# A state-space convolution feeding a 4-bit FFN: filler matmuls, one late load and one kernel product moved in the lead

## Chip, cores and metric

One core of a Trainium2 chip runs the whole kernel. The metric is device time in microseconds (us) for one execution; the time of a kernel is the median of its runs. A profiled execution gives a trace, whose span runs from the first to the last instruction.

## What is computed

`x` has 32 batch rows, 64 heads and 1024 positions. Each head has a long convolution kernel, made from a diagonal state-space model with 64 states; the masked input is convolved with it, and the result goes through a gated FFN whose weights are 4-bit integers with a scale for each group of 128 inputs. The output is added to `x`.

```python
def _L0_cond_ref(u, length, log_dt, C, log_A_real, A_imag, D):
    dtA = A * dt[:, None]
    P = dtA[:, :, None] * jnp.arange(length)
    Cs = Cc * (jnp.exp(dtA) - 1.0) / A
    kernel = 2.0 * jnp.einsum('hn,hnl->hl', Cs, jnp.exp(P)).real
    u_m = u * mask[:, None, :]
    y = irfft(rfft(u_m, 2 * L) * rfft(kernel, 2 * L))[..., :L]
    y = y + u_m * D[:, None]
    return y * mask[:, None, :]

def _L0_ffn_ref(x, ...):
    gate = x2 @ Wg          # 1024 -> 2752, dequantized from 4 bits
    up = x2 @ Wu
    inter = gate * jax.nn.sigmoid(gate) * up
    return (inter @ Wd).astype(jnp.float16)

x = x + _L0_ffn_ref(_L0_cond_ref(x, ...), ...)
```

## The kernel before

**Tiling and stages.** The 64 heads are four blocks of 16. A block's convolution gives 512 rows of FFN input, on which the FFN then runs: gate and up products (`gu_one`, `gu_pair`), the gated product, and the down product (`dn_pair`). From some 60 us on, convolution heads of the next block are woven between FFN matmuls. The part before that, in which block 0 is made ready and convolved, is called the lead here; the change touches only the lead.

**From coefficients to a convolution kernel.** For a group of heads, `phase_tables` (L183 to L210) makes tables of sines: DVE computes the phases (L192 to L204), ACT takes the sine (L207) and the square (L209). `kernel_factors` (L213 to L224) turns them into two factors `e1t` and `e2t` on DVE (L218 to L223). `make_kernel` (L421) multiplies them on PE: a matmul with the tap `D` (L425), then one small float32 matmul for each head (L427), which the trace shows as two passes each. The product `kq` is split into two float16 parts `kb` by ACT (L430) and DVE (L431), and two DMAs on ACT's queue write them to `kpad` in DRAM (L433).

**Toeplitz loads.** `toeplitz` (L513) issues on SP's queue one 512 KB load for each head (L525), which reads `kpad` with overlapping rows, so that each partition holds a shifted copy of the kernel. It can't begin before the two writes of its group have landed. The destination is a piece of a tile that is free at that time, so in the profile the same load is called `w<-kpad` (heads 0 to 7 and 15), `t<-kpad` or `ihl<-kpad`.

**Input of the convolution.** Four heads share one 512 KB load of `u`. `conv_fetch` issues those of heads 0 to 15 at the very start; `conv_split` (L492) makes two float16 parts, `uh` by a cast on ACT and `ul` by a subtract on DVE (L497). For heads 16 and up `conv_load` (L500) issues the load on SP (L503), then the cast (L507) and the subtract (L510).

**One head of the convolution.** `conv_head` (L531) issues 24 matmuls (L548): eight diagonals, and for each of them high by `uh`, high by `ul`, and low by `uh`. It is a generator that yields after each diagonal, so a head has eight steps and block 0 has 128. Two heads share a PSUM tile `cq`; after the second, DVE masks it into `y` (L560), ACT casts it to `xh` (L563), and POOL, or DVE for the last pair of a block, subtracts to give `xl` (L565). The FFN products read `xh` (L664) and `xl` (L665) and rescale their accumulator between groups (`rescale_two`, L635 to L640).

**The lead, in order.** A loop over the first two groups of four heads (`for k, h0 in enumerate((0, 4))`) makes tables, factors, kernel and Toeplitz loads, then calls `busy`, then `conv_split`. `busy` issues n filler matmuls (L884) of 128x128x128 in float32, whose result nobody reads; each is two passes on PE. Heads 8 to 15 get their tables and factors behind the loop. Then block 0 is convolved, and at given steps of its 128 other work is issued: `events` maps a step to a function, `unpack_it` unpacks the first FFN weights (two SP loads `qgu` and `z`, L578 and L579, then DVE L584, POOL L590, and ACT or DVE), and `group_it` prepares heads 24 to 31. At the events, step 7 makes the kernel of heads 8 to 15 and the factors of 16 to 23, 63 issues fillers, 56 makes the gate/up scale ratios (`scale_ratios`, L405 to L419: ACT copy, then DVE L413 to L418), 87 loads `u` of heads 16 to 19, and 75 makes the kernel of heads 16 to 23. Behind block 0, `second` makes the down-projection's ratios, issues the Toeplitz loads of heads 16 to 21 and convolves heads 16 to 31.

**What sets the order.** The tile framework places each instruction in its engine's queue by priority, in about the order in which the code issues it. `mark(key, inst)` remembers an instruction, and `with after(key)` places what is issued inside it behind the remembered one on its queue. The keys `"act"`, `"dve"` and `"sp"` stand for the latest marked instruction of that engine. SP's queue and ACT's queue issue DMAs; the framework rotates eight semaphores over the DMAs of both.

Of the kernel before, what the change touches and what calls it, by code (L numbers as in the profile page):

```python
# [17 lines left out]
ALU = mybir.AluOpType  # L18
# [164 lines left out]
def phase_tables(nc, side, pool, co, cst, h0, nh):  # L183
    ts, tt, stt = nc.vector.tensor_scalar, nc.vector.tensor_tensor, nc.vector.scalar_tensor_tensor
    hs = slice(h0, h0 + nh)
    idx = cst[:, 0:64].unsqueeze(1).to_broadcast([128, nh, 64])
    per = lambda a, n: a[:, hs].unsqueeze(2).to_broadcast([128, nh, n])
    t = lambda name, n: pool.tile([128, nh, n], F32, name=name)
    off1, off2 = cst[:, 64:65], cst[:, 65:66]

    ph, pl = t("ph", 64), t("pl", 64)
    tt(ph, per(co["wh"], 64), idx, ALU.mult)  # L192
    yield
    side.tensor_tensor(pl, per(co["wl"], 64), idx, ALU.mult)
    r1, r2 = t("r1", 64), t("r2", 32)
    yield
    ts(r1, ph, off1, MAGIC, ALU.add, ALU.add)
    ts(r2, ph[:, :, 32:], off2, MAGIC, ALU.add, ALU.add)
    yield
    stt(r1, r1, MAGIC, ph, ALU.subtract, ALU.subtract)  # L200
    stt(r2, r2, MAGIC, ph[:, :, 32:], ALU.subtract, ALU.subtract)
    yield
    stt(r1, r1, off1, pl, ALU.subtract, ALU.subtract)
    stt(r2, r2, off2, pl[:, :, 32:], ALU.subtract, ALU.subtract)  # L204
    yield
    for r in (r1, r2):
        nc.scalar.activation(r, r, AF.Sin, scale=3.1415925)  # L207
    for r in (r1, r2):
        sq_op = nc.scalar.activation(r, r, AF.Square, scale=1.4142135623730951)  # L209
    return r1, r2, sq_op  # L210


def kernel_factors(nc, pool, co, xd, s1, s2, h0, nh):  # L213
# [34 lines left out]
def every(gen):  # L248
    for _ in gen:
        pass  # L250
# [8 lines left out]
class Core:  # L259
# [183 lines left out]
    def tables(self, pool, h0, nh):  # L443
        held = h0 >= 24
        steps = phase_tables(self.nc, self.nc.vector, pool, self.co, self.cst, h0, nh)
        while True:
            try:
                with self.after("dve" if held else None), self.after("act" if held else None):
                    next(steps)
            except StopIteration as done:  # L450
                self.tab, sq_op = done.value[:2], done.value[2]
                break
            self.dve(800)
            yield
        self.mark(("sq", h0), sq_op)
        self.act(5000)
        yield
        yield from self.pause(5000)
# [33 lines left out]
    def conv_split(self, k, after, last="e"):  # L492
        u, uh, ul = self.us[k]
        with self.after(("sq", after)):
            self.nc.scalar.copy(uh, u)
        with self.after((last, after)):
            self.nc.vector.tensor_tensor(ul, u, uh, ALU.subtract)  # L497
        self.us[k] = uh, ul

    def conv_load(self, h0):  # L500
        nc = self.nc
        u = self.cv.tile([128, 8, 4, B], F32, name="u", bufs=1)
        self.mark("sp", nc.sync.dma_start(u.rearrange("p c h b -> p (c h b)"), self.io["xF"][h0 // 4]))  # L503
        uh = self.cv.tile([128, 8, 4, B], F16, name="uh")
        ul = self.cv.tile([128, 8, 4, B], F16, name="ul")
        with self.after("act"):
            nc.scalar.copy(uh, u)  # L507
        self.act(1000)
        with self.after("dve"):
            nc.vector.tensor_tensor(ul, u, uh, ALU.subtract)  # L510
        self.dve(1200)
        return uh, ul
# [323 lines left out]
def tile_ssm_ffn(ctx, tc, io):  # L836
    nc = tc.nc
    c = Core(ctx, tc, io)
# [14 lines left out]
    kg = kg_stack.enter_context(tc.tile_pool(name="kg", bufs=1))  # L853
# [27 lines left out]
    def busy(h0, n):  # L881
        e1, e2 = (e.rearrange("p h n -> p (h n)") for e in c.fac[h0])
        for _ in range(n):
            nc.tensor.matmul(c.psum("wq", "b")[:, 0, :128], e1, e2, start=True, stop=True)  # L884

    for k, h0 in enumerate((0, 4)):
        every(c.tables(tables, h0, 4))
        every(c.factors(kg, h0, 4, xd[0][:, h0:h0 + 4]))
        c.make_kernel(kg, h0, 4, "b")
        for h in range(h0, h0 + 4):  # L890
            c.t0[h] = c.toeplitz(h)
        busy(h0, 8 - 4 * k)
        c.conv_split(k, h0)
    every(c.tables(kg, 8, 8))
    every(c.factors(kg, 8, 8, xd[1]))
    c.masks()
    tc.no_sync_barrier()
# [35 lines left out]
    def load_16():  # L933
        c.us[4] = c.conv_load(16)

    events = {7: kernel_8, 63: lambda: busy(4, 10), 56: ratios_gu, 87: load_16, 75: lambda: c.make_kernel(kg, 16, 8, "b")}
    for i, _ in enumerate(c.conv(0)):
        if i in events:
            with c.after("dve" if i == 56 else None):
                events[i]()  # L940
        if i in (32, 40, 48, 56, 64, 72, 104, 116, 124):
            next(unpack_it)
        if i in (80, 86, 92, 98, 104, 110):
            next(group_it)
# [175 lines left out]
```

## Time and profile before

| | us |
|---|---|
| median of 3 runs | 1079.41 (1079.26 to 1080.23) |
| the profiled execution | 1076.19 |
| its span | 1074.4 |
| PE busy in the span | 1025.0 (95%) |
| DVE, ACT, POOL busy | 804.7, 773.7, 243.9 |
| mean granted TensorE clock | 0.997 |

The profiled execution's own time is 1.8 us more than its span and 3.2 us less than the median of the runs. In a row of the timeline the first number is the start, the second the duration from the first to the last of the xN instructions in the row; in brackets stand the idle time of the engine before it and what ended it. In a table by stretches each engine has its busy time, with the number of instructions after it.

### The profile page before, as it was taken

What the parts mean: (1) busy time and instruction counts of PE and PEld (TensorE: products, weight loads), DVE (VectorE), ACT (ScalarE), POOL (GpSimd) and SP (SyncE); (2) the same over time, 40 slices, a digit from 0 to 9 for tenths busy, and PEclk for the clock granted to TensorE, in tenths of its full rate; (3) what the DMA queues carried; (4) which work ended last, traced back from release to release, by engine and by line L of the source; (5) the groups of instructions that cost most, each with busy time, mean ns of one, the idle gap of its engine ahead of it and who ended that gap; (6) DMA issues with size and microseconds to landing.
All of it is one profiled execution on the core that took longest, in us unless ns stands there. A gap on an engine that the chain in (4) does not pass through costs nothing.

```text
span 1074.4 us, 15424 instructions
## 1 busy us (share of the span) xinstructions
PE 1025.0 (95%) x5854; PEld 512.6 (48%) x5854; DVE 804.7 (75%) x938; ACT 773.7 (72%) x1031; POOL 243.9 (23%) x272
## 2 busy tenths in 40 slices
PE   3989999999899999997999999999999999999996
PEld 3867444444344445663665444444444444444442
DVE  8964888888977786678456777777778777777775
ACT  5767778787677787778577777666666667778774
POOL 0334123232332333230112112222221111102002
PEclk9999999999999999999999999999999999999998
DMA  6976321111111424455752011000000002325002
GB/s 196 332 243 211 100 69 40 40 59 40 49 50 58 139 90 156 152 180 190 238 167 99 30 38 42 20 20 20 18 13 20 20 20 79 118 72 166 37 1 79
DMA packets 52099, 99.76 MB, mean 93 GB/s; under 512 B 9524, under 2 KB 11444, under 8 KB 52024
## 3 DMA queue, kind: packets, MB, share of 16 engines
q1 hardware_dynamic: 38888, 70.09, 20.1%
q0 software_dynamic: 5280, 17.31, 4.3%
q10 hardware_dynamic: 7856, 11.37, 3.6%
q8 instruction: 46, 0.75, 0.3%
q14 instruction: 29, 0.24, 0.1%
HBM read 78.99 MB, written 19.76 MB: 92 GB/s over the span
## 4 chain that ended last, share of the span: by engine, by line
PE 81%; DVE 7%; ACT 5%; DMA 3%; issue 2%; POOL 1%; DVEq 0%; SPq 0%; ACTq 0%; POOLq 0%
PE chq L687 23%; PE chq L688 22%; PE chq L732 12%; PE chq L733 12%; PE cq L548 6%; PE chq L664 2%; PE chq L665 2%; DMA t<-kpad 2%; ACT chq L640 1%; DVE chq L618 1%; DVE v L700 1%; ACT chq L620 1%; DMA ihl<-kpad 1%; ACT sg L695 1%; POOL spill L310 0%
## 5 line engine op out<-in xcount | busy, mean ns | idle before, releaser
L687 PE MATMUL chq<-xh,w 128*128 128x512 f16 x1216 | 459.4, 379 | 7.2 <-DVE chq L618 2.1
L688 PE MATMUL chq<-xl,w 128*128 128x512 f16 x1216 | 457.6, 379 | 0.0
L618 DVE TENSOR_SCALAR chq<-chq,gur 128x1024 f32<-128x1024 f32 x261 | 333.3, 1290 | 93.4 <-PE chq L688 91.8
L620 ACT ACTIVATE chq<-chq,gur 128x1024 f32<-128x1024 f32 x285 | 304.2, 1085 | 86.9 <-PE chq L688 84.4
L640 ACT ACTIVATE chq<-chq,dnr 128x512 f32<-128x512 f32 x358 | 232.8, 661 | 68.6 <-PE chq L733 62.8
L732 PE MATMUL chq<-ihl,wd 128*128 128x512 f16 x672 | 253.0, 379 | 8.9 <-ACT chq L640 5.2
L733 PE MATMUL chq<-ihl,wd 128*128 128x512 f16 x672 | 252.9, 379 | 0.0
L637 DVE TENSOR_TENSOR chq<-chq,dnr 128x1024 f32<-128x1024 f32 x141 | 173.1, 1230 | 81.0 <-PE chq L733 80.2
L688 PEld LDWEIGHTS <-w 128*128 128x128 fp8e4 x1216 | 118.6, 98 | 154.6 <-issue 18.5
L687 PEld LDWEIGHTS <-w 128*128 128x128 fp8e4 x1216 | 118.7, 98 | 146.7 <-issue 1.1
L310 POOL TENSOR_TENSOR ihl<-v,ihl 128x512 f16<-128x512 f32 x42 | 48.3, 1150 | 364.0 <-ACT ihl L629 364.0
L733 PEld LDWEIGHTS <-wd 128*128 128x128 fp8e4 x672 | 65.4, 97 | 81.0 <-issue 18.2
L548 PEld LDWEIGHTS <-t 128*128 128x128 f16 x1152 | 81.3, 98 | 38.7 <-DMA t<-kpad 5.8
L732 PEld LDWEIGHTS <-wd 128*128 128x128 fp8e4 x672 | 65.4, 98 | 67.2 <-issue 0.8
L548 PE MATMUL cq<-uh,t 128*128 128x256 f16 (+3 forms) x720 | 91.1, 226 | 4.1 <-DMA t<-kpad 4.0
L565 POOL TENSOR_TENSOR xl<-y,xh 128x512 f16<-128x512 f32 x28 | 36.4, 1301 | 161.0 <-ACT xh L563 161.0
L548 PE MATMUL cq<-ul,t 128*128 128x256 f16 (+3 forms) x360 | 71.6, 225 | 0.0
L629 ACT CAST ihl<-v 128x512 f16<-128x512 f32 x42 | 25.9, 617 | 58.7 <-DVE v L700 55.3
L700 DVE SCALAR_TENSOR_TENSOR v<-chq,gul,sg 128x1024 f32<-128x1024 f32 x38 | 48.6, 1280 | 17.2 <-PE chq L688 11.3
L310 POOL TENSOR_TENSOR spill<-v,spill 128x512 f16<-128x512 f32 x42 | 48.8, 1161 | 14.2 <-ACT spill L629 13.9
L640 ACT ACTIVATE chq<-chq,gur 128x512 f32<-128x512 f32 x66 | 43.2, 661 | 11.0 <-PE chq L665 9.8
L590 POOL TENSOR_TENSOR w<-w,z 128x256 int32<-128x256 int32 x42 | 31.6, 772 | 81.2 <-DVE w L584 76.9
(249 smaller groups left out, 812.5 us busy)
## 6 DMA issues: line engine op xcount, KB each, us to landing
t<-kpad SPq DMA_DIRECT2D x48, 512.0 KB, 4.3
spill<-spill POOLq DMA_DIRECT2D x42, 256.0 KB, 2.7
ihl<-spill ACTq DMA_DIRECT2D x42, 256.0 KB, 2.7
z<-zc SPq DMA_DIRECT2D x29, 256.0 KB, 3.7
u<-xF SPq DMA_DIRECT2D x12, 512.0 KB, 3.9
xr<-xT SPq DMA_DIRECT2D x12, 512.0 KB, 4.5
out<-xr POOLq DMA_DIRECT2D x24, 256.0 KB, 2.9
w<-qgu SPq DMA_DIRECT2D x21, 256.0 KB, 4.8
```

The source lines that it names most:

```text
L310: self.nc.gpsimd.tensor_tensor(out, a, b, op)
L548: nc.tensor.matmul(q[:, d:, h % 2, :], t0[:, lw, 128 * d:128 * d + 128], uu[:, 0:8 - d, h % 4, :], start=(d == 0 and k == 0 and h % 2 == 0 ...
L565: split.tensor_tensor(xl[:, :, ts], yv, xh[:, :, ts], ALU.subtract)
L618: self.mark("dve", self.nc.vector.tensor_scalar(q, q, col, None, ALU.mult))
L620: self.mark("act", self.nc.scalar.activation(q, q, AF.Copy, scale=col))
L637: self.mark("dve", self.nc.vector.tensor_tensor(q, q, cols.to_broadcast([128, 2, 512]), ALU.mult))
L640: self.mark("act", self.nc.scalar.activation(q[:, k], q[:, k], AF.Copy, scale=cols[:, k]))
L687: nc.tensor.matmul(q[:, b], lw, xh[:, g, :], start=(g == 0), stop=False, skip_group_check=True)
L688: nc.tensor.matmul(q[:, b], lw, xl[:, g, :], start=False, stop=(g == GH - 1), skip_group_check=True)
L700: nc.vector.scalar_tensor_tensor(v, q, last, self.sg.pop(ct - 21), ALU.mult, ALU.mult)
L732: nc.tensor.matmul(q[:, j], lw, self.ihl[:, g, 0], start=(g == 0), stop=False, skip_group_check=True)
L733: nc.tensor.matmul(q[:, j], lw, self.ihl[:, g, 1], start=False, stop=False, skip_group_check=True)
```

## The change

Six edits, all in the lead:

- The first set of filler matmuls in the loop over the two groups has 5 calls instead of 8; the second stays at 4 (5 - 1 for 8 - 4).
- The split of the input of heads 4 to 7 (ACT cast, DVE subtract) is no longer issued at the end of the loop's second turn, but between the tables and the factors of heads 8 to 15. For that, `phase_tables` also returns its last DVE instruction (L204), which is marked as `("r", h0)`, and the subtract is placed behind that of heads 8 to 15.
- The load of `u` for heads 16 to 19 is placed behind the latest marked SP load, which at that place in the code belongs to the Toeplitz loads of heads 8 to 15 or to an unpack's `z`.
- The fillers at step 63 have 4 calls instead of 10.
- The gate/up ratios are made at step 80 instead of 56.
- The kernel product of heads 16 to 23 is made at step 66 instead of 75.

On SP's queue this moves the load of `u` and one `qgu` block, which stood between the Toeplitz loads of heads 7 and 8, behind those of heads 8 to 15 and two further pairs of `qgu` and `z`.

```diff
@@ phase_tables
-    stt(r2, r2, off2, pl[:, :, 32:], ALU.subtract, ALU.subtract)
+    last = stt(r2, r2, off2, pl[:, :, 32:], ALU.subtract, ALU.subtract)
...
-    return r1, r2, sq_op
+    return r1, r2, sq_op, last
@@ Core.tables
                 self.tab, sq_op = done.value[:2], done.value[2]
+                self.mark(("r", h0), done.value[3])
@@ conv_split
-        with self.after((last, after)):
+        with self.after(last if isinstance(last, tuple) else (last, after)):
             self.nc.vector.tensor_tensor(ul, u, uh, ALU.subtract)
@@ conv_load
-        self.mark("sp", nc.sync.dma_start(u.rearrange("p c h b -> p (c h b)"), self.io["xF"][h0 // 4]))
+        with self.after("sp" if h0 == 16 else None):
+            self.mark("sp", nc.sync.dma_start(u.rearrange("p c h b -> p (c h b)"), self.io["xF"][h0 // 4]))
@@ the loop over the first two groups
-        busy(h0, 8 - 4 * k)
-        c.conv_split(k, h0)
+        busy(h0, 5 - k)
+        if k == 0:
+            c.conv_split(k, h0)
     every(c.tables(kg, 8, 8))
+    c.conv_split(1, 4, ("r", 8))
     every(c.factors(kg, 8, 8, xd[1]))
@@ the events of block 0
-    events = {7: kernel_8, 63: lambda: busy(4, 10), 56: ratios_gu, 87: load_16, 75: lambda: c.make_kernel(kg, 16, 8, "b")}
+    events = {7: kernel_8, 63: lambda: busy(4, 4), 80: ratios_gu, 87: load_16, 66: lambda: c.make_kernel(kg, 16, 8, "b")}
     for i, _ in enumerate(c.conv(0)):
         if i in events:
-            with c.after("dve" if i == 56 else None):
+            with c.after("dve" if i == 80 else None):
                 events[i]()
```

## The prediction

> **What bounds the kernel now.** I began with the chain of waits. It says that the span ends on TensorE work, so only what lets PE begin its unbroken stretch sooner counts.
>
> ```profile
> span 1074.4 us, 15424 instructions
> ...
> PE 81%; DVE 7%; ACT 5%; DMA 3%; issue 2%; POOL 1%; DVEq 0%; SPq 0%; ACTq 0%; POOLq 0%
> ```
>
> Second, PE's busy time stretch by stretch, to see where that stretch begins.
>
> ```profile
> 57.40:60.80 3.40, 1.55 (x26) 1.42 (x24) 2.05 (x4) 3.40 (x7) 3.40 (x4) 1.00 0.98 243
> ...
> 63.00:106.00 43.00, 42.79 (x439) 30.14 (x437) 23.50 (x31) 31.35 (x48) 13.31 (x13) 1.00 0.68 229
> ...
> 1064.40:1067.70 3.30, 1.18 (x4) 0.28 (x3) 2.55 (x5) 1.35 (x2) 1.80 (x2) 1.00 0.00 0
> 1067.80:1070.00 2.20, 0.00 (x0) 0.00 (x0) 1.51 (x2) 0.00 (x0) 0.36 (x1) 0.50 0.77 288
> ```
>
> The second column is PE's busy time, the last three are granted clock, DMA share and GB/s. From 63 to 106 us PE is busy 42.79 of 43.00. So the gain or loss is the shift of the moment, about 63, from which PE is never short of work. The lead before it is the third view, PE's timeline; waits stand in brackets.
>
> ```profile
> 17.46 0.64 PE L427 MATMUL kq<-e2t,e1t 128*32 128x32 f32 x8 [13.48 <-DVE e1t L223]
> 18.03 3.78 PE L884 MATMUL wq<-e2t,e1t 128*128 128x128 f32 x16
> ...
> 22.30 0.64 PE L427 MATMUL kq<-e2t,e1t 128*32 128x32 f32 x8
> 22.87 2.08 PE L884 MATMUL wq<-e2t,e1t 128*128 128x128 f32 x8
> 24.74 2.65 PE L548 MATMUL cq<-ihl,w 128*128 128x256 f16 x24
> ...
> 28.74 0.69 PE L427 MATMUL kq<-e2t,e1t 128*32 128x32 f32 x16 [0.81 <-DVE e1t L223]
> 29.36 11.11 PE L548 MATMUL cq<-ihl,w 128*128 128x256 f16 x168
> 40.32 2.48 PE L884 MATMUL wq<-e2t,e1t 128*128 128x128 f32 x20
> 43.44 2.77 PE L548 MATMUL cq<-ihl,t 128*128 128x256 f16 x36 [0.64 <-DMA t<-kpad]
> ...
> 56.38 1.68 PE L548 MATMUL cq<-ihl,w 128*128 128x256 f16 x24
> 59.91 0.28 PE L548 MATMUL cq<-uh,t 128*128 128x256 f16 x1 [1.85 <-DMA t<-kpad]
> ...
> 62.97 0.38 PE L665 MATMUL chq<-xl,w 128*128 128x512 f16 x1
> ```
>
> Fillers are the L884 rows. The waits that matter are head 8 for its Toeplitz load (`t<-kpad`) and head 16 for its own; the first up-projection matmul on `xl` (62.97) opens the unbroken stretch. Fourth, the SP queue, since loads set both waits, and two DVE rows.
>
> ```profile
> 32.22 0.48 SPq L503 DMA_DIRECT2D u<-xF  x1
> 32.73 0.96 SPq L578 DMA_DIRECT2D w<-qgu  x1
> ...
> 55.85 1.40 SPq L525 DMA_DIRECT2D t<-kpad  x3
> ```
>
> ```profile
> 52.99 1.21 DVE L510 TENSOR_TENSOR ul<-u,uh 128x1024 f16<-128x1024 f32 x1
> ...
> 61.73 1.04 DVE L565 TENSOR_TENSOR xl<-y,xh 128x512 f16<-128x512 f32 x1
> ```
>
> **Part 1, the first fillers (8 to 5; the second set stays at 4).** Each call is two passes; 16 take 3.78 us to the next row, 0.213 a pass at the half pace PE has there, so 6 passes are 1.28 us. The product of heads 4 to 7 starts at 21.02 instead of 22.30; its factors are ready at 20.75, so it doesn't wait. Its two `kpad` writes leave 1.28 earlier (21.99 for 23.27), but landing is another matter: the four 512 KB loads of heads 0 to 3 are in flight, and these writes took 5.4 us to land (28.58 and 29.13), while those of heads 0 to 3, on idle DMA engines, took 1.5 to 2 (18.43 to 20.40). So the loads of heads 4 to 7, which wait for the writes, come 0 to 1.28 sooner. I take 0.6: nearer to the row with the loads in front, which is the same situation.
>
> The Trainium skill, "DMA: Bandwidth & Descriptors", section "Queues, rings and completion order", says that each DMA engine goes round-robin between queue rows, a packet at a time. By it the writes, on another queue than the loads, would not stand behind them and the whole 1.28 would come through; the 5.4 us row speaks against it.
>
> **Part 2, the split of heads 4 to 7 behind the tables of heads 8 to 15.** One ACT cast and one DVE subtract (1.20 us at 20.68) leave the front of DVE's queue. The factors of heads 8 to 15, the 0.81 us wait at 28.74, come about 1.4 sooner, and that product at about 27.7. Heads 1 to 7 start near 28.3, but then run into the landings of loads 4 to 7 (the last at 38.73, less Part 1). The subtract is needed at head 4, some 5 us later: it costs nothing, and if DVE were full there it would cost its 1.2.
>
> **Part 3, `u` of head 16 and one `qgu` block out from between loads 7 and 8.** With the DMA engines saturated, successive 512 KB loads land 1.36 us apart (46.10, 47.46, 48.81), so `qgu` (256 KB) is worth 0.68, and `u` about 1.43. Head 8's load lands 2.11 sooner plus Part 1's 0.6, at about 40.7 in place of 43.4. The fillers behind head 7 go from 20 passes to 8: 12 by 0.111 is 1.33 us, and they now end before the load lands, where they cost nothing. One thing is unexplained: head 8 landed 2.55 after the `qgu` in front, where 1.36 is the pace. If this 1.2 us slip is tied to the old order, it goes as well: 0 to 1.2; nothing in the rows decides, and I take half, 0.6. Block 0 then ends near 54.4 (58.06 before).
>
> **Part 4, what goes late in exchange.** `u` is issued behind heads 8 to 15 and two `qgu`/`z` pairs. In the trace each transfer of the SP and ACT queues is issued after the landing of the one eight before it, so it leaves when head 14's load lands (about 49.0 by the slow reading) and lands behind head 15 (1.36), four 256 KB blocks (2.72) and itself (1.43): 54.5, where it had been 40.16. Its cast (1.04) and subtract (1.21) follow: 56.8; the Toeplitz load of head 16 lands about 57.2. So head 16 starts near 57.3 and not 59.91, because the DMA engines no longer stand idle from 54.2 to 57. But PE sits idle 2.9 us before it instead of 1.85.
>
> This cast and subtract now hold up their engines, which they didn't before. Behind the subtract on DVE stand the reductions L201 to L204, an unpack and the last `y` (59.78 before, now 58.4); behind the cast on ACT the `xh` of heads 12 and 13 (and POOL's `xl` after it), two unpacks, the sines, then the last `xh`, at about 61.1 for 61.09.
>
> **Part 5, kernel product of heads 16 to 23 nine steps sooner, ratios behind it.** 18 PE matmuls, an ACT and a DVE evacuation and two DMAs move; the two writes land some 4 us sooner, which releases head 16's load early enough that the queue, not the product, sets it. The gate/up ratios (about 4 us of DVE between 39 and 48.8) go later, into DVE's 51 to 58. The reciprocal of the down-projection's ratios (L417, 1.24 us at 62.69, behind the last `xl`) now stands ahead of that `xl`. So `xl` comes at 62.4 to 62.75 and ends hardly sooner than in the trace before.
>
> **The sum.** At the moment when `xl` opens the stretch, PE has done more: 19 convolution matmuls (24 take 1.53 us, so 1.21) and one L664 (0.21) are moved ahead: 1.4, with 0.2 from `xl`: 1.6. On ACT and DVE the next `xh` and a rescale change places with what the first accumulations wait for; by the 0.17 to 0.34 us waits on these lines I take back 0.4: 1.2. Parts 1 and 3 bring the load of `u`, and all behind it, 0.6 and 0.6 sooner; nearly all of it reaches `xl`: 1.1. Together −2.3 us: the profiled execution would go from 1076.19 (span 1074.4 and 1.8 around it) to 1073.9. The median of the runs stands 3.2 us above that execution, by something that the lead doesn't touch, so I forecast 1079.4 − 2.3 = 1077.1. The unknown terms give it 0.9 (neither the 0.6s nor any of 0.2) to 3.6: 1075.8 to 1078.5. No gain can exceed what was removed plus PE's waits in the lead: 2.6 of fillers and 4.8 of idle, 7.4.
>
> **Rivals.** *All of it* (chance 0.17): the writes land 1.28 sooner, the slip is gone and nothing is given back: 1.6 + 1.28 + 1.2 = 4.1, 1075.3. For it: DMA idle at 54 to 57 is visibly there to be used. Against: the 5.4 us landing, and `xl` behind the reciprocal.
>
> *Hidden* (0.15): the late `u` uses up what the early loads win, `xl` stands where it was, and the moved matmuls only trade places with waits: 1079.0. For it: ACT's last `xh` comes out unchanged.
>
> *The clock is lost* (0.22), the one on the slower side. Place: the idle 2.9 us before head 16, about 54.4 to 57.3. The profile shows that a 3.30 us stretch with 1.18 us of PE work was followed by a clock of 0.50, and that one of 3.40 with 1.55 kept 1.00. The new stretch may hold only 0.5. Price: at the start, half pace (24 matmuls take 2.65 us at 24.74 and 1.68 at 56.38) lasted from 17.46 to 26.70, 9.24 us, in which PE loses 4.6; net −2.3 + 4.6 = +2.3, 1081.7. It decides once less than about 1.2 to 1.5 us of work is left in a stretch; against it, stretches may be cut so that the idle is split between two, and half pace is partly hidden while heads 16 and 17 wait for `xl` anyway.
>
> On this the Trainium skill, "TensorE: Matmul & The Clock Gate", section "Why this matters for your kernels", warns of "No PE-idle gaps >~3µs between matmul bursts", and its Part 1 gives a free-running window of 3413 ns. By the rule a gap of 2.9 us would pass; by the row with 1.18 us busy it need not, and the fillers were what filled such gaps.
>
> **How the numbers follow.** A measurement of this kernel tells about 0.2% (2.16 us) from no change. The likeliest case has 0.46, of which 0.27 lies beyond 2.16; with 0.17 that is 0.44 faster. Same: the other 0.19 and 0.15, 0.34. Slower: 0.22. The range runs from the full case, 1075.0, to the lost clock, 1081.9.
>
> **What would show it.** Right: the product of heads 4 to 7 at 21.0; head 8 near 40.7; head 16 near 57.3 behind `ul`, not `t`; clock 1.00 throughout. Wrong: loads 4 to 7 landing as before (Part 1 nothing), head 8 still 2.5 us behind its predecessor (no slip to win), a granted clock of 0.50 near 57 (third rival), or the first `xl` matmul at 62.97 with no more matmuls ahead of it.

## The result, and the profile after

| | before | after |
|---|---|---|
| median of 15 runs each, us | 1078.77 | 1081.23 |
| lowest, highest, us | 1076.69, 1083.90 | 1079.25, 1085.61 |
| profiled execution, us | 1076.19 | 1083.28 |
| its span, us | 1074.4 | 1081.5 |
| mean granted clock in it | 0.997 | 0.991 |

The change makes the kernel slower: ratio 1.0029, 95% interval 1.0018 to 1.0039, where 1077.1 us had been forecast. The two profiled executions lie on opposite sides of their medians (2.6 us below, 2.1 above), so their 7.1 us apart overstate the loss; the medians are 2.5 apart.

First PE's timeline of the changed kernel; the fillers now have line 886, the convolution 550, the first up-projection products 666 (`xh`) and 667 (`xl`).

```profile
24.52 3.06 PE L550 MATMUL cq<-ihl,w 128*128 128x256 f16 x24 [0.84 <-DMA w<-kpad]
...
28.36 0.69 PE L427 MATMUL kq<-e2t,e1t 128*32 128x32 f32 x16
28.98 11.02 PE L550 MATMUL cq<-ihl,w 128*128 128x256 f16 x168
39.85 1.14 PE L886 MATMUL wq<-e2t,e1t 128*128 128x128 f32 x8
43.03 1.04 PE L550 MATMUL cq<-ihl,t 128*128 128x256 f16 x9 [2.04 <-DMA t<-kpad]
...
56.62 1.68 PE L550 MATMUL cq<-ihl,w 128*128 128x256 f16 x24
61.57 0.28 PE L550 MATMUL cq<-uh,t 128*128 128x256 f16 x1 [3.27 <-DMA t<-kpad]
...
64.85 1.00 PE L666 MATMUL chq<-xh,w 128*128 128x512 f16 x2 [0.23 <-POOL w L592]
...
66.84 0.38 PE L667 MATMUL chq<-xl,w 128*128 128x512 f16 x1
...
73.57 0.61 PE L425 MATMUL kq<-ihl,cst 1*32 1x256 f32 x2
```

Head 8 starts at 43.03, where 43.44 was before and 40.7 was forecast. Head 16 starts at 61.57 (59.91 before, 57.3 forecast), after an idle 3.27. The first `xl` product stands at 66.84 instead of 62.97. Other work is ahead of it, so a fairer mark is the kernel product of heads 24 to 31, the L425 row at 73.57: it stood at 71.12 before. By it the lead has lost 2.45 us, about the difference of the medians. That is for this pair of executions: in a second profile of the kernel before, further down, the row stands at 70.26, and the loss would be 3.3.

```profile
71.12 0.61 PE L425 MATMUL kq<-ihl,cst 1*32 1x256 f32 x2
```

Second, why head 8 hardly moved: SP's queue with the two kernel writes of ACT's queue, and SP's waits between 27 and 45 us, of the changed kernel.

```profile
28.13 2.00 SPq L527 DMA_DIRECT2D w<-kpad  x4
37.77 2.06 SPq L527 DMA_DIRECT2D t<-kpad  x3
```

```profile
29.49 1.11 ACTq L433 DMA_DIRECT2D kpad<-kb  x2
```

```profile
SPq L527 <- DMA kpad<-kb: 13.2, 2, 7.6
```

The same before:

```profile
29.19 2.98 SPq L525 DMA_DIRECT2D w<-kpad  x4
35.90 1.55 SPq L525 DMA_DIRECT2D t<-kpad  x3
```

```profile
30.56 1.03 ACTq L433 DMA_DIRECT2D kpad<-kb  x2
```

```profile
SPq L525 <- DMA kpad<-kb: 8.9, 2, 6.7
```

The numbers of a wait are us in total, times, longest. Head 8's load waits for the two kernel writes of heads 8 to 15, 7.6 us at the longest, and these writes went out among the loads of heads 4 to 7. With `u` and the `qgu` block gone from this place SP just waits longer, and the DMA engines run dry, as the table by stretches shows (clock, DMA share and GB/s are the last three columns):

```profile
37.80:38.40 0.60, 0.60 (x17) 0.60 (x15) 0.60 (x2) 0.59 (x3) 0.60 (x2) 1.00 0.12 27
38.40:41.80 3.40, 2.59 (x36) 2.36 (x31) 2.45 (x5) 3.40 (x7) 3.40 (x4) 1.00 0.71 188
...
41.82:45.23 3.41, 2.20 (x28) 1.56 (x29) 2.41 (x3) 1.33 (x3) 1.80 (x3) 1.00 1.01 312
45.23:48.64 3.41, 3.41 (x30) 3.09 (x31) 0.41 (x1) 2.04 (x3) 0.92 (x1) 0.50 1.05 401
...
58.88:62.30 3.42, 0.73 (x8) 0.70 (x9) 3.42 (x5) 0.29 (x1) 2.29 (x2) 1.00 1.04 391
62.30:65.71 3.41, 3.18 (x25) 2.21 (x23) 3.38 (x7) 3.09 (x6) 2.60 (x4) 0.50 1.06 396
```

It shows the clock too: 0.50 for 3.41 us from 45.23, behind a stretch with 2.20 us of PE work and the idle before head 8, and from 62.30, behind 3.4 us with 0.73 of PE work. The kernel before had neither.

Third, DVE in front of the first up-projection products:

```profile
52.71 1.25 DVE L417 RECIPROCAL ihl<-ihl 128x88 f32<-128x88 f32 x2
...
54.43 1.20 DVE L417 RECIPROCAL ihl<-ihl 128x88 f32<-128x88 f32 x2
...
58.44 1.21 DVE L512 TENSOR_TENSOR ul<-u,uh 128x1024 f16<-128x1024 f32 x1
...
62.79 0.68 DVE L562 TENSOR_TENSOR y<-cq,mask 128x512 f32<-128x512 f32 x1
...
64.31 1.25 DVE L417 RECIPROCAL ihl<-ihl 128x176 f32<-128x176 f32 x1
65.48 0.63 DVE L567 TENSOR_TENSOR xl<-y,xh 128x512 f16<-128x512 f32 x1
```

From 49.24 on DVE has no gap, and the last `y`, whose input block 0 had finished at 58.3, comes 4.5 us later (before: 58.06 and 59.78, 1.7 later). Behind it the down-projection's reciprocal goes ahead of `xl`.

Behind the lead the order is the old one. This execution loses a further 0.7 at 109.7 (a Toeplitz load that lands 0.80 late for PE) and 3.9 around two more stretches at 0.50 (it is 2.8 behind the kernel before at 397 us and 6.7 from 523 on):

```profile
506.03:509.44 3.41, 3.41 (x10) 1.21 (x9) 2.74 (x6) 0.81 (x3) 0.00 (x0) 0.50 0.58 205
519.68:523.09 3.41, 3.41 (x30) 3.03 (x28) 0.00 (x0) 0.00 (x0) 0.00 (x0) 0.50 0.22 82
```

The kernel before has the same idle there (PE busy 2.15 of 4.00 us from 500 to 504) and kept 1.00. Stretches at 0.50 stand near this place in two other kernels' traces as well (split and product from 503.20, fillers back from 514.12), so this part is taken here for chance of an execution.

### The profile page after: what moved, and what is told of

It is laid out like the page before. It is cut to its first block, busy times and chain, and to the rows that moved or that the text cites. A ratio compares the mean times of both kernels' runs of the same rounds, so it can differ in the third digit from the quotient of the medians.

```text
span 1081.5 us, 15387 instructions
## 1 busy us (share of the span) xinstructions
PE 1029.0 (95%) x5836; PEld 513.9 (48%) x5836; DVE 804.9 (74%) x938; ACT 773.7 (72%) x1031; POOL 241.8 (22%) x272
## 4 chain that ended last, share of the span: by engine, by line
PE 78%; DVE 8%; ACT 5%; DMA 4%; issue 3%; POOL 1%; DVEq 0%; ACTq 0%; POOLq 0%; SPq 0%
PE chq L689 22%; PE chq L690 22%; PE chq L734 12%; PE chq L735 12%; PE cq L550 6%; PE chq L666 2%; PE chq L667 2%; DMA t<-kpad 2%; ACT chq L642 1%; DVE chq L620 1%; DVE v L702 1%; ACT chq L622 1%; DMA kpad<-kb 1%; ACT sg L697 1%; DMA out<-xr 1%
## 5 line engine op out<-in xcount | busy, mean ns | idle before, releaser
L550 PEld LDWEIGHTS <-t 128*128 128x128 f16 x1152 | 84.5, 101 | 43.0 <-DMA t<-kpad 9.9
L567 POOL TENSOR_TENSOR xl<-y,xh 128x512 f16<-128x512 f32 x28 | 34.1, 1218 | 168.5 <-ACT xh L565 168.5
L631 ACT CAST ihl<-v 128x512 f16<-128x512 f32 x42 | 25.9, 617 | 58.4 <-DVE v L702 55.0
L697 ACT ACTIVATE sg<-chq,gul 128x1024 f32<-128x1024 f32 x38 | 42.3, 1113 | 10.7 <-PE chq L690 9.8
```

Source lines behind the costliest of these rows:

```text
L550: nc.tensor.matmul(q[:, d:, h % 2, :], t0[:, lw, 128 * d:128 * d + 128], uu[:, 0:8 - d, h % 4, :], start=(d == 0 and k == 0 and h % 2 == 0 ...
L697: nc.scalar.activation(sg, q, AF.Silu, scale=last)
```

## The experiments

Each was timed against the kernel before in shared runs (29 to 35 of the kernel before, 6 to 12 of each other). Two theories were set against each other. Order: the late `u` is the loss. Clock: the missing fillers are. Four runs undo or do one part alone.

**`u` early again, all else changed.**

```diff
-        with self.after("sp" if h0 == 16 else None):
+        with self.after(None):
```

> The changed kernel with one part undone: the load of u of head 16 is no longer held behind the Toeplitz loads of heads 8 to 15, so that u and one qgu block stand between the loads of heads 7 and 8 again. Order theory (the late u is the loss: it delays head 16's load, and what it vacates was only filling the time in which the kernel writes of heads 8 to 15 land): head 16 starts at 59.9 or sooner instead of 61.57, PE's wait before it is under 2 us instead of 3.27, and the kernel loses its 2.5 us and some more: ratio to before 0.998 to 1.000. Clock theory (the missing fillers are the loss, through dropped clock): still slower, ratio 1.001 to 1.003, with 0.50 granted somewhere between 40 and 66 us.

Ratio 1.0020 (1.0009 to 1.0030). The places came as the order theory says: head 8 at 40.58, head 16 at 57.30. But the kernel is still slower. The last `y` starts at 59.38, 4.5 us behind the end of block 0 at 54.9, and the first L667 at 63.02 although head 16 had started 2.6 us sooner. So a second delay stands behind the first. But this trace doesn't show where the time goes: by the fairer mark (the L425 row, at 69.75) its lead lost nothing, and at 1075.88 us it is the fastest of the kernel's twelve executions, whose median is 1079.44. Granted 0.50 from 57.05 to 60.46 was seen, as the clock theory has it.

**Fillers back, all else changed.**

```diff
-        busy(h0, 5 - k)
+        busy(h0, 8 - 4 * k)
...
-63: lambda: busy(4, 4)
+63: lambda: busy(4, 10)
```

> The changed kernel with the fillers back at 8, 4 and 10 calls, all else changed. Order theory: about as slow as the changed kernel, ratio to before 1.002 to 1.003, head 16 at 61 to 62 behind a wait of over 3 us; the stretch of clock 0.50 at 45 may go, but what it cost was hidden before head 16. Clock theory: no 0.50 between 40 and 66 us and the loss gone, ratio 0.999 to 1.001.

Ratio 1.0033 (1.0020 to 1.0045): nothing is won back, and the filler theory alone falls. A stretch at 0.50 still stands in its lead, from 63.56 to 66.98. Nor was the order theory right in detail, since head 16 started at 57.84, not 61. PE then waited for DVE and ACT. PE and DVE in this kernel:

```profile
63.77 1.01 PE L666 MATMUL chq<-xh,w 128*128 128x512 f16 x2 [3.39 <-ACT xh L565]
66.81 0.45 PE L667 MATMUL chq<-xl,w 128*128 128x512 f16 x1
```

```profile
55.87 1.22 DVE L512 TENSOR_TENSOR ul<-u,uh 128x1024 f16<-128x1024 f32 x1 [1.33 <-ACT uh L509]
...
61.71 0.68 DVE L562 TENSOR_TENSOR y<-cq,mask 128x512 f32<-128x512 f32 x1
```

Head 16 is 2.1 us sooner than before the change and the first `xl` product 3.8 later: what binds is the last `y`, then `xh`.

**The late `u` alone, on the kernel before.**

```diff
+        with self.after("sp" if h0 == 16 else None):
```

> The kernel before with one part of the change alone: the load of u of head 16 behind the Toeplitz loads of heads 8 to 15. Order theory: head 8 starts less than 0.8 us sooner than 43.44, head 16 starts 1.5 us or more later than 59.91, ratio to before 1.002. Clock theory: all fillers are there, so ratio 0.999 to 1.001.

Ratio 1.0018 (1.0009 to 1.0028), as the order theory expected, but not by its path: head 16 started at 59.26, sooner than before. DVE shows the path:

```profile
56.90 1.44 DVE L511 TENSOR_TENSOR ul<-u,uh 128x1024 f16<-128x1024 f32 x1 [0.92 <-ACT uh L508]
...
61.62 0.68 DVE L561 TENSOR_TENSOR y<-cq,mask 128x512 f32<-128x512 f32 x1
```

The subtract waits for a late `u` with the rest of DVE's queue behind it: L204, then on ACT the sines, then L221, then the last `y`, 5.0 us behind the end of block 0 (56.6). That is what the prediction had named for these queues, with a smaller price (4.0 us, from 54.4 to 58.4).

**Fewer fillers alone, on the kernel before.**

```diff
-        busy(h0, 8 - 4 * k)
+        busy(h0, 5 - k)
...
-63: lambda: busy(4, 10)
+63: lambda: busy(4, 4)
```

> The kernel before with one part of the change alone: 5 filler calls instead of 8 in the first set and 4 instead of 10 at step 63. Order theory: head 8 and head 16 still wait for their loads and start within 0.5 us of 43.4 and 59.9, ratio to before 0.999 to 1.001, whether or not a stretch of 0.50 appears. Clock theory: 0.50 granted between 40 and 66 us and ratio 1.002.

Ratio 1.0018 (1.0005 to 1.0030): slower, and not by a stretch of 0.50 between 40 and 66, of which there was none. Head 8's load left at 39.50 instead of 35.90 and head 16 started at 61.54. The reason is in the first rows: head 0 still ran at half pace, and three of the four loads of heads 4 to 7 went out ahead of the first kernel write of heads 8 to 15 (29.92), all four ahead of the second (30.72).

These four left a new theory, in two parts. Writes: head 8's load waits for writes that queue behind whatever loads left first. DVE: late ratios and a late `ul` push the last `y` and `xl`. Four more runs tested it.

**Kernel product and ratios alone, on the kernel before.**

```diff
-    events = {..., 56: ratios_gu, ..., 75: lambda: c.make_kernel(kg, 16, 8, "b")}
+    events = {..., 80: ratios_gu, ..., 66: lambda: c.make_kernel(kg, 16, 8, "b")}
```

> The kernel before with one part of the change alone: the kernel product of heads 16 to 23 at step 66 and the gate/up ratios at step 80. DVE theory (the ratios, moved into the 48 to 57 us in which DVE also has the tables of heads 24 to 31 and the split of head 16, push the last y of block 0 and put a 1.24 us reciprocal ahead of the last xl, so PE waits for xh and xl even when head 16's load is early): head 16 starts at 59 or sooner, but the last y starts at 60.5 or later and the first L665 at 63.5 or later; ratio to before 1.001 to 1.002. Load theory (only head 16's load counts): head 16 starts some 2 us sooner and the kernel is faster, ratio 0.998.

Ratio 1.0021 (1.0011 to 1.0031). Head 16 at 58.71, last `y` at 62.18, first L665 at 67.15, and a ratio at the upper edge of what was expected: as the DVE theory has it, and against the load theory, since head 16's load was sooner and the kernel slower.

**Ratios back, all else changed.**

```diff
-    events = {..., 80: ratios_gu, ...}
+    events = {..., 56: ratios_gu, ...}
```

> The changed kernel with the gate/up ratios back at step 56, all else changed. DVE theory: the last y starts within 2.5 us of the end of block 0 instead of 4.5 us behind it, and the kernel gains 1 to 2 us on the changed one: ratio to before 1.001 to 1.002. Load theory: the load of head 16 still sets the start, ratio 1.003 as for the changed kernel.

Ratio 1.0022 (1.0013 to 1.0031), the upper edge of what was expected and not apart from 1.0029. The last `y` came 2.0 us behind block 0, as foreseen, but block 0 itself ended at 60.82. Head 8 wasn't the reason, since it started at 43.02, as in the changed kernel (43.03). PE then stood still before the product of heads 16 to 23:

```profile
47.18 1.06 PE L427 MATMUL kq<-e2t,e1t 128*32 128x32 f32 x16 [2.58 <-DVE e1t L223]
```

The factors that it waits for now stand behind the ratios on DVE, while the product is still at its earlier step; and from 47.19 the clock was 0.50 for a stretch. With one loss taken away another stands there.

**Split and kernel product alone.** The kernel before with the split of heads 4 to 7 moved as in the change, and

```diff
-    events = {..., 75: lambda: c.make_kernel(kg, 16, 8, "b")}
+    events = {..., 66: lambda: c.make_kernel(kg, 16, 8, "b")}
```

> The kernel before with the split of heads 4 to 7 behind the tables of heads 8 to 15 and the kernel product of heads 16 to 23 at step 66; fillers, u and ratios as before. Write theory (head 8's load can't leave before the two kernel writes of heads 8 to 15 have landed, and each 512 KB load issued ahead of a write costs it about 1.4 us): with all fillers the clock is full early, the writes leave at about 28.9 and 29.7 and stand ahead of loads 6 and 7, head 8's load is issued 0.5 to 2.5 us sooner than at 35.90 and head 16 starts at 57 to 59; the last y isn't pushed; ratio to before 0.997 to 0.999. If instead PE's later work sets the time, ratio 1.000.

Ratio 1.0001 (0.9991 to 1.0011). Head 16 did come sooner (58.55) and the last `y` didn't (59.90): the gain was expected and is not there. These two parts together neither lose nor win; so the loss of product and ratios points to the ratios. No run has the product without the split or the ratios, so that isn't shown.

**The kernel before, profiled again.**

> The kernel before, unchanged, for a second profile. Ratio 1.000 within 0.001. If the places in the lead are set by a race between the kernel writes and the loads, head 8 and head 16 may start up to 2 us away from 43.44 and 59.91; if not, they start within 0.3 us of these.

Ratio 0.9998 (0.9987 to 1.0009). Head 8 at 42.49 and head 16 at 58.87, each 1.0 sooner than in the first profile, with the same code: the places in the lead vary by a microsecond between executions. A place in a single trace is read with this in mind.

Three runs then split what was left.

**First filler set alone.**

```diff
-        busy(h0, 8 - 4 * k)
+        busy(h0, 5 - k)
```

> The kernel before with the first filler set alone cut from 8 to 5 calls; 4 and 10 stay. Clock theory for the start (the first fillers bring the full clock; cut, it comes at 26 to 33 us instead of 21 to 27, so head 0 and the product of heads 8 to 15 run at half pace while the loads of heads 4 to 7 leave sooner, and the kernel writes of heads 8 to 15 end up behind all four of them): head 8's load is issued at 37.5 to 39.5 instead of 34.8 to 35.9, ratio to before 1.001 to 1.002. If fillers are only a cost: 0.999 to 1.000.

Ratio 1.0007 (0.9994 to 1.0020), unclear. Its mechanism shows: head 0 at half pace (24 matmuls 3.06 us), head 8's load at 37.98, inside the expected 37.5 to 39.5. Head 8 nevertheless started at 42.18, straight behind the fillers and without a wait, sooner than before.

**Second filler set alone.**

```diff
-63: lambda: busy(4, 10)
+63: lambda: busy(4, 4)
```

> The kernel before with the fillers at step 63 alone cut from 10 to 4 calls; 8 and 4 stay. They end before head 8's load lands, so nothing is gained; PE only idles some 1.3 us more before head 8. Expected 0.9995 to 1.0005, and 1.001 if that idle costs the clock (a stretch of 0.50 between 42 and 50 us).

Ratio 1.0015 (1.0003 to 1.0027), where nothing was expected, though the interval begins close to that. No stretch of 0.50 stands between 42 and 50 in the profiled execution; its only one in the lead is at 28.22 to 31.63, ahead of the step that was changed. What these fillers are worth is not explained by a trace here; the trace's head 16 (59.22) and first L665 (62.85) stand as before.

**Ratios alone.**

```diff
-    events = {..., 56: ratios_gu, ...}
+    events = {..., 80: ratios_gu, ...}
```

> The kernel before with the gate/up ratios alone moved from step 56 to 80. DVE theory: this is the part that made the run with product and ratios slow; the last y starts at 61 or later, the first L665 at 63.5 or later, ratio to before 1.001 to 1.002. If it was the product: ratio 1.000.

Ratio 1.0008 (0.9997 to 1.0020): the places came as expected (last `y` at 61.32, first L665 at 65.29), the time is under what they say, and the interval includes no change, so this run decides neither way. With the product sooner (the earlier run) the same ratios cost 1.0021.

**A candidate.** Split and product as above, and the tables of heads 24 to 31 and the last unpack steps at earlier steps, so that DVE and ACT are clear when block 0 ends.

```diff
-        if i in (32, 40, 48, 56, 64, 72, 104, 116, 124):
+        if i in (32, 40, 48, 56, 64, 72, 96, 104, 112):
             next(unpack_it)
-        if i in (80, 86, 92, 98, 104, 110):
+        if i in (72, 77, 82, 87, 92, 98):
             next(group_it)
```

> A candidate that beats both: the split of heads 4 to 7 and the kernel product of heads 16 to 23 moved as in the change, fillers, u and ratios as before, and the tables of heads 24 to 31 and the last three steps of the weight unpacking spread over earlier steps (72, 77, 82, 87, 92, 98 and 96, 104, 112). With the DVE theory the last y then follows the end of block 0 within 1.5 us, xh comes about 1 us sooner and the first L665 at about 61.3: ratio to before 0.998 to 0.9995. If loads alone set the start: 1.000.

Ratio 0.9989 (0.9979 to 0.9999), median 1076.14 us against 1077.54: the only one that beat the kernel before, by 0.1%, with an interval that ends just under 1 and overlaps that of its base, split and product (1.0001). The mark moved with it. Its DVE and PE:

```profile
56.90 0.69 DVE L561 TENSOR_TENSOR y<-cq,mask 128x512 f32<-128x512 f32 x1 [1.20 <-PE cq L549]
...
59.28 1.21 DVE L566 TENSOR_TENSOR xl<-y,xh 128x512 f16<-128x512 f32 x1
60.42 1.24 DVE L417 RECIPROCAL ihl<-ihl 128x176 f32<-128x176 f32 x1
```

```profile
58.23 0.28 PE L549 MATMUL cq<-uh,t 128*128 128x256 f16 x1 [1.45 <-DMA t<-kpad]
...
61.24 0.38 PE L666 MATMUL chq<-xl,w 128*128 128x512 f16 x1
```

DVE now waits for PE before the last `y`, not the other way round.

**All executions together.** The place where the prediction failed first is the race of writes and loads. From the traces, with the pace of head 0 (24 matmuls), the issue of the last of the four loads of heads 4 to 7, that of the second kernel write of heads 8 to 15, and that of head 8's load; then the fairer mark of the lead (the L425 row) and the ratio of the runs:

| kernel | head 0, us | last load out | second write out | head 8's load out | mark | ratio |
|---|---|---|---|---|---|---|
| before | 2.65 | 31.70 | 31.27 | 35.90 | 71.12 | 1 |
| before, again | 1.69 | 30.98 | 30.54 | 34.77 | 70.26 | 0.9998 |
| candidate | 1.69 | 32.03 | 29.17 | 34.30 | 69.39 | 0.9989 |
| split and product | 1.69 | 30.72 | 29.41 | 35.15 | 70.74 | 1.0001 |
| fillers back | 1.69 | 30.46 | 29.72 | 35.44 | 73.60 | 1.0033 |
| `u` early again | 2.72 | 30.51 | 29.24 | 33.43 | 69.75 | 1.0020 |
| late `u` alone | 1.69 | 31.06 | 30.55 | 36.68 | 72.04 | 1.0018 |
| product and ratios | 1.69 | 31.27 | 31.23 | 37.72 | 73.87 | 1.0021 |
| second fillers alone | 1.69 | 30.72 | 30.75 | 36.99 | 71.01 | 1.0015 |
| after | 3.06 | 29.56 | 30.29 | 37.77 | 73.57 | 1.0029 |
| first fillers alone | 3.06 | 29.77 | 30.35 | 37.98 | 70.73 | 1.0007 |
| ratios back | 3.06 | 29.71 | 30.61 | 38.19 | 73.20 | 1.0022 |
| ratios alone | 2.79 | 30.59 | 31.39 | 39.37 | 73.14 | 1.0008 |
| fewer fillers alone | 3.06 | 29.94 | 30.72 | 39.50 | 72.06 | 1.0018 |

Where the second write left behind the last load, head 8's load left at 37.0 to 39.5; where it left ahead of it, at 33.4 to 37.7. All five kernels with 5 first calls ran head 0 at half pace; of the nine with 8, two did. Mark and ratio mostly go together: a mark of 72 or later goes with 1.0018 or more, except for the ratios alone, and a sooner one with 1.0007 or less, except for `u` early again and the second fillers alone. In these exceptions a single trace doesn't show the loss, or shows one that the runs don't confirm.

The mean granted clock over all runs sorts the same kernels another way. It was 0.9924 for the changed kernel (15 runs), 0.9932 to 0.9943 for the six others that have the late `u`, the late ratios or both (6 to 12 runs each), and 0.9953 to 0.9959 for the kernel before (29, 35 and 35 runs), the candidate, split and product, and all three kernels in which only fillers were cut. So the cut fillers, which the clock theory blamed, do not lower the mean by themselves; the late `u` and the late ratios go with a lower one. One stretch of 3.41 us at 0.50 is 0.0016 of the mean (1.7 of 1079), so the changed kernel has about two more of them in a run. One such stretch (split and product, at 503.20) put the work behind it 1.67 us later. An estimate of their price over the runs: among the 35 runs of the kernel before taken with the last experiments 0.001 of clock goes with 0.5 us, so 0.0035 with some 1.7 us of the 2.5 to 3. That is a correlation, not an experiment.

## Why the prediction was wrong

**The direction and the size.** Forecast −2.3, measured +2.5 us in the median. The slower side had been given 0.22, through a lost clock. The range reached to 1081.9 for its sake and so holds the time, but the likeliest case was wrong. That the time lies near the lost clock's 1081.7 is in part luck, since the loss is not made up as that case has it (below).

**Part 3 is the step that failed first: "Head 8's load lands 2.11 sooner plus Part 1's 0.6".** It counted only the transfers in front of head 8's load and left out what that load itself waits for, the two kernel writes of heads 8 to 15; SP's waits on `kpad<-kb` (8.9 us) told of it before the change. In the changed kernel the second write landed at 37.69 and the load left at 37.77, 1.87 later than before (35.90). In all four traces that record this landing the load left 0.07 to 0.08 behind it. With `u` and `qgu` gone from its front it then took 5.2 us instead of 7.5 to land, so of the 2.7 us (2.11 and 0.6) 0.4 was left, and the DMA share had fallen to 0.12 in the wait. With the first set cut and `u` in its old place (first fillers alone) the load left at 37.98 and PE had no wait for it; there `u` and `qgu` were only filling. Where the writes stayed early the order did win: the load landed at 41.40 with the late `u` alone and at 39.51 with the fillers back, for 43.4. Part of that was hidden, as the fillers at step 63 held PE until 42.95 and 42.13.

The 1.2 us "slip" is not tied to the old order: with `u` early again, which has that order, head 8 started 1.4 us behind the landing of the `qgu` in front (40.58 and 39.19). And the end of block 0, forecast 3.7 us sooner, is more than its terms, 2.11, 0.6 and 0.6, add up to; some 0.3 has no row.

**Part 1's term had the wrong sign for head 8's load.** The product of heads 4 to 7 did start at 21.03 and its loads left 1.06 sooner (28.13 for 29.19), within the 0 to 1.28 given. But the fillers were also what brought the clock: head 0 ran at 3.06 us for 24 matmuls, the next product came at 28.36, not 27.7, and the writes that follow it lost the race to those sooner loads: the third and fourth load left 2.14 us sooner than before, the writes 1.07. With the fillers back, and all else as in the change, the first write left ahead of all four loads (28.93) and landed in 1.8 us. With the first set cut, in five executions of five, head 8's load left at 33.4 to 39.5, in four of these at 37.8 or later. In time the first set alone is not shown to cost anything (1.0007, unclear).

**Part 4 named the mechanism and undersized it.** "Behind the subtract on DVE stand ... the last `y` (59.78 before, now 58.4)": it came at 62.79, 4.4 later. `u` landed at 56.9 instead of 54.5, and from there to the last `y` it took 5.9 us instead of 3.9. The late ratios are not needed for that, since the late `u` alone, without them, took 5.8. It cost 1.0018.

**Part 5 costed the ratios at nothing**, "into DVE's 51 to 58". DVE had no room there: of what stood in front of the last `y` in the changed kernel, 4.7 us were theirs (L413 to L418 from 49.84 on: 0.33, 1.49, 1.25, 1.20, 0.46). Alone they gave 1.0008, unclear; with the product sooner 1.0021, where split and product alone gave 1.0001. So their cost in time is shown only together with the product. The reciprocal ahead of `xl` was seen and came so (64.31 ahead of 65.48).

**Part 2** was right as far as it goes: with the split moved the product of heads 8 to 15 came at 26.82 to 27.40 in three traces with all the first fillers, for 28.01 and 28.74 before. In time the split was run only with the product (1.0001).

**The rivals.** The lost clock was right that it would appear behind the wait before head 16: 3.4 us with 0.73 of work, then 0.50. Its price was not 4.6: each lost stretch lasted 3.41 us, so 1.7 at most (1.67 measured), and it took about two more of them per run, before head 8 as well. The rule quoted from the Trainium skill, "TensorE: Matmul & The Clock Gate", section "Why this matters for your kernels", that gaps above about 3 us cost the clock, agrees with the 3.27 us gap here; the stretch at 45.23 followed a gap of 2.04 us only, with 2.20 of 3.41 us busy, so a shorter gap than the rule names was enough, and so was more work than the prediction's 1.2 to 1.5 us. And gaps of 2.66, 2.97 and 3.04 us before head 16 (late `u`, first fillers and fewer fillers, each alone) kept 1.00. So neither the length of a gap nor that threshold decides by itself, and what does stays open.

**On the arbitration rule** of the Trainium skill, "DMA: Bandwidth & Descriptors", section "Queues, rings and completion order", that each DMA engine goes round-robin between queue rows: the changed kernel's first write, out at 29.49 behind three loads, took 6.9 us and landed at 36.39, 0.17 ahead of the load issued last before it (36.56), and the candidate's, out at 28.40 ahead of all four, 1.8. The measurement decides: here a write mostly waits for the loads issued ahead of it.

**Not additive.** Late `u`, fewer fillers, and product with ratios gave 1.0018, 1.0018 and 1.0021 alone, and 1.0029 together; undoing `u`, the fillers or the ratios alone left 1.0020 to 1.0033. A reading that fits, though no run shows it by itself: each holds the same moment, the first products on `xh` and `xl`, by another path, and the longest counts.

**Still open:** why the second filler set alone costs 1.0015, and how much of the loss is clock and how much the late start; no kernel was tried that keeps the clock up by other work in those waits, none has the product alone, and none the first set of fillers back with all else changed.

## What to carry to other kernels

A transfer that stands in front of a late one is a cost only if the late one could have gone: look first at what its issue waits for. Filler matmuls whose result nobody reads may be carrying the clock for the next product, and with it an order between queues. When several paths meet within 2 us, undoing one part of a loss shows little; follow the one instruction where they meet (here the last `y`) in every run.

## What was not expected of the hardware

For a small write behind big loads, tenths of a microsecond decide: the first 16 KB write landed in 1.8 to 2.0 us where it was issued up to 0.4 ahead of four 512 KB loads (three kernels), in 2.7 to 3.8 us behind one or two of them (four executions), and in 4.75 to 7.6 us behind three or four (seven kernels). And the kernel before took from 1076.7 to 1083.9 us in 15 runs; in 35 others its mean granted clock lay between 0.991 and 0.998.
